# Scan rows of 16 channels by eight states, third-order permutation at the sums, and scores in 32x128 tiles

## The chip, the cores and the metric

The kernel runs on one core of a Trainium2 chip. The metric is the device time of one execution in microseconds (us), from the first to the last instruction. The engines run their own instruction streams in order and wait for each other by semaphores: PE (TensorE, matmuls; PEld are its weight loads), DVE (VectorE), ACT (ScalarE), POOL (GpSimd) and SP, which only issues DMA transfers. All data is fp32, and an fp32 matmul appears in the trace as two passes, each with a weight load.

## The reference, cut to what matters

Two layers act on `x` of 4 images of 64 x 64 tokens with 128 channels. Layer 0 adds a selective scan (Mamba) in three orders of the tokens: forward, backward, and a "sliced" order in which 16 slices of 256 tokens are interleaved. Layer 1 adds an attention block of 16 heads of 8 channels, in which queries, keys and values are one and the same tensor, and a mixture of 64 experts in which each expert picks tokens.

```
def selective_scan(u, delta, A, B, C):             # 256 channels d, 16 states n, 4096 tokens
    def step(h, inp):
        u_, de_, b_, c_ = inp
        dA = jnp.exp(de_[..., None] * A)
        h = h * dA + (de_ * u_)[..., None] * b_[:, None, :]
        y = jnp.einsum('bdn,bn->bd', h, c_)
        return (h, y)

def mamba_dir(xz, ...):                            # once for each of the three orders
    x = silu(causal_conv1d(x, conv_w, conv_b))
    ...
    delta = jax.nn.softplus(jnp.einsum('dr,brl->bdl', dt_w, dt_raw) + dt_b[None, :, None])
    y = selective_scan(x, delta, A, Bm, Cm)
    y = y + Dp[None, :, None] * x
    return y * silu(z)

scores = jnp.einsum('bhsd,bhtd->bhst', q, q) / np.sqrt(D)    # 16 heads, 4096 x 4096 tokens, D = 8
attn = jax.nn.softmax(scores, axis=-1)
ctx = jnp.einsum('bhst,bhtd->bhsd', attn, q)
```

## The kernel before, in words

**Inputs of the scan** (`Inputs`). For each image, order and chunk of 1024 tokens, `of_chunk` computes the convolution on PE (L357), the SiLU on ACT (L368), the projections (L380, L399), softplus (ACT for Abs, Relu, Exp and Ln at L404 to L411, one DVE pass at L413 that makes `s`, three matmuls at L419 that add the parts, one DVE add at L421) and `du = delta * u` (L425). It writes `delta`, `du`, `u` and the rows of B and C to DRAM through POOL's queue (L340, L385). For the sliced order it makes a second SiLU in permuted order (L370), so that `u` lies in DRAM as the sums will be needed. L302 permutes the image itself.

**The scan** (`Scans.of_image`). The 256 channels by 16 states of one image do not fit 128 partitions. One *step* `s` takes 8 channels: partition p = 8 n + d holds state n of channel d. A chunk of 1024 tokens has 32 steps (k = 0 to 7, j = 0 to 3), an image has 3 orders x 4 chunks x 32 = 384 steps. Each step

- loads `delta` and `du` of its 8 channels, each repeated over 16 states (L480, 512 KB each, on SP's queue; for image 0 `du` is on ACT's);
- takes exp(delta * A) in place on ACT (L492);
- multiplies `du` by the B rows in place (L498), scans along the tokens with `tensor_tensor_scan` (L501), and multiplies by the C rows back into the `du` tile (L508), all on DVE. In the sliced order (order 2) L508 reads and writes in permuted order;
- copies the last column for the next chunk on POOL (`ends`, L502);
- sums over the states on PE (`total`, L514), with a selection matrix `sel` for each j. Four steps make 32 channels; then `out` adds D * u on DVE (L525) and POOL writes the rows to DRAM (L530, L536, and L539 for order 2).

Loads are emitted two steps ahead (`AHEAD`), exps one, and the sums of a group of four steps in the second and third step of the next group. `delta` has 3 buffers, `du` 8, `h` 3.

**Attention** (`Attention.loop`). One image has 1024 rounds (4 head groups j x 8 query blocks of 512 x 32 key blocks of 128). A round computes the scores of four heads in two pairs. Each pair has its own PSUM tile `s` of two banks, and there are three such tiles. For each head the keys are cut into four blocks of 32, so that a matmul (L829) contracts 32 rows (the other heads are masked off in the queries) and yields 32 of 128 key rows: 16 matmuls in a round, each on a 32x32 tile of the array. ACT takes the exp of each pair (L836), and four matmuls with 32 columns each add the values (L845). Round i emits scores(i + 1), then values(i), and then `beside(i)`.

**What runs beside what.** The order of instructions is written by generators. In the *fill* (L1300 to L1305) the scan of image 0 and the inputs of all four images take turns. Then `opening` reads the sums of image 0 and prepares its attention, with some of image 1's scan. In the loops of images 0 to 2, `beside` inserts the scan of the next image, and what follows and precedes attention for the neighbouring images. The loop of image 3 has only such other work, no scan.

Of the kernel before, what the change touches and what calls it, by code (L numbers as in the profile page):

```python
# [16 lines left out]
P = 128  # L17
# [8 lines left out]
NC = L // T  # L26
NB = DI // 8
# [105 lines left out]
def scan_weights(nc, const, load, load_ps, ident, in_proj_w, out_proj_w, dirs):  # L133
# [16 lines left out]
    for i, d in enumerate(dirs):  # L150
# [26 lines left out]

        w["A"] = const["all"].tile([P, NB], F32, name=f"A{i}")
        a_log = d["A_log"].rearrange("(k d) n -> n d k", d=8)
        for n in range(NS):  # L180
            nc.scalar.dma_start(out=w["A"][n * 8 : n * 8 + 8, :], in_=a_log[n])
        nc.scalar.activation(w["A"], w["A"], AF.Exp)
        nc.vector.tensor_scalar_mul(w["A"], w["A"], -1.0)

# [10 lines left out]
        ws.append(w)  # L195
    return w_z, w_out, ws


class Inputs:
# [3 lines left out]
    def __init__(self, tc, ctx, x, w_z, ws, cols, dram, ident):  # L203
# [20 lines left out]
        nc.vector.tensor_scalar_mul(self.minus, ident, -1.0)  # L224
        self.made, self.sz, self.normed, self.sliced, self.gated = {}, {}, {}, {}, {}
# [101 lines left out]
    def of_chunk(self, b, order, c):  # L327
# [34 lines left out]
        kept = u  # L362
        if order == 2:

            kept = self.piece.tile([P, 2, T], F32, tag="us", name=f"uk_{key}")
        for m in range(2):
            bias = w["conv_b"][:, m : m + 1]
            nc.scalar.activation(u[:, m, :], banks[m], AF.Silu, bias=bias)  # L368
            if order == 2:
                nc.scalar.activation(  # L370
                    kept[:, m, :].rearrange("p (i j) -> p j i", i=SLICES),
                    banks[m].rearrange("p (j i) -> p j i", i=SLICES), AF.Silu, bias=bias,
                )
            self.leave()
        keep("u", kept)
# [37 lines left out]
        nc.vector.tensor_scalar(s, e, 1.0, -1.0, ALU.add, ALU.add)  # L413
# [17 lines left out]
class Scans:  # L431
# [6 lines left out]
    def __init__(self, tc, ctx, ws, ident, bank, dram):  # L438
# [7 lines left out]
        self.sel = const.tile([P, 4, 32], F32, name="sel")  # L446
        nc.vector.memset(self.sel, 0.0)
        for j in range(4):
            nc.vector.tensor_reduce(
                self.sel[:, j, 8 * j : 8 * j + 8], ident.rearrange("p (n d) -> p d n", d=8),  # L450
                mybir.AxisListType.X, ALU.add,
            )
        self.sums, self.steps, self.did = {}, {}, set()

    def of_image(self, b, made, queue=None):
# [8 lines left out]
        def rows_of(order, c):  # L464
            for i, name in enumerate(("B", "C")):
                t = self.rows.tile([P, T], F32, tag=name, name=f"{name}_{b}_{order}_{c}")
                nc.sync.dma_start(out=t, in_=made[b, order, c]["bc"][i].unsqueeze(1).to_broadcast([NS, 8, T]))
                spread[order, c, name] = t
            ends[order, c] = self.small.tile([P, NB], F32, tag="ends", name=f"ends_{b}_{order}_{c}")

        def load(s):
            order, c, k, j = steps[s]
            if k == j == 0:
                rows_of(order, c)
            at = 8 * (4 * k + j)
            for name, bufs in (("delta", 3), ("du", 8)):
                t = self.deep.tile([P, T], F32, tag=name, bufs=bufs, name=f"{name}_{b}_{s}")
                src = made[b, order, c][name][at : at + 8]
                by = queue if queue is not None and name == "du" else nc.sync
                by.dma_start(out=t, in_=src.unsqueeze(0).to_broadcast([NS, 8, T]))  # L480
                tiles[name, s] = t
# [6 lines left out]
        def exp(s):  # L488
            order, c, k, j = steps[s]
            at = 4 * k + j  # L490
            t = tiles["delta", s]
            nc.scalar.activation(t, t, AF.Exp, scale=self.ws[order]["A"][:, at : at + 1])  # L492

        def step(s):
            order, c, k, j = steps[s]
            at = 4 * k + j
            dA, dB = tiles.pop(("delta", s)), tiles["du", s]
            nc.vector.tensor_mul(dB, dB, spread[order, c, "B"])  # L498
            h = self.deep.tile([P, T], F32, tag="h", name=f"h_{b}_{s}")
# [3 lines left out]
            into, C_rows = dB, spread[order, c, "C"]  # L503
            if order == 2:

                into = dB.rearrange("p (i j) -> p j i", i=SLICES)
                h, C_rows = (t.rearrange("p (j i) -> p j i", i=SLICES) for t in (h, C_rows))
            nc.vector.tensor_mul(into, h, C_rows)  # L508

        def total(s, y):  # L510
            order, c, k, j = steps[s]
            hC = tiles.pop(("du", s))
            for g in range(4):
                nc.tensor.matmul(  # L514
                    y[32 * g : 32 * g + 32, : T // 4], self.sel[:, j, :], hC[:, 256 * g : 256 * g + 256],
# [3 lines left out]
        def out(s, y):  # L519
# [3 lines left out]
            o = self.rows.tile([P, T // 4], F32, tag="o", name=f"o_{b}_{s}")  # L523
            into = o[:, ::-1] if order == 1 else o
            nc.vector.scalar_tensor_tensor(  # L525
                into, u, self.ws[order]["D"][:, k : k + 1], y[:, : T // 4], ALU.mult, ALU.add
            )
# [4 lines left out]
            for g in range(4):  # L532
# [4 lines left out]
                else:  # L537
                    n = T // SLICES
                    nc.gpsimd.dma_start(  # L539
                        out=to.rearrange("p (i j) -> p i j", i=SLICES)[:, 4 * g : 4 * g + 4, c * n : (c + 1) * n],  # L540
                        in_=rows.rearrange("p (i j) -> p i j", i=4),
# [57 lines left out]
class Attention:  # L599
# [202 lines left out]
    def loop(self, b, beside):  # L802
# [17 lines left out]
        def scores(i):  # L820
# [3 lines left out]
            for pair in range(2):  # L824
                s_ps = self.ps_s.tile([P, 2, QB], F32, tag="s", name=f"s_{b}_{i}_{pair}")
                for k in range(2):
                    at = 32 * (2 * pair + k)
                    for r in range(0, P, 32):
                        nc.tensor.matmul(  # L829
                            s_ps[r : r + 32, k, :],  # L830
                            qT[at : at + 32, kc * P + r : kc * P + r + 32],
                            queries[j, qb][at : at + 32, :],
                            start=True, stop=True,
                        )
# [566 lines left out]
```

## Time and profile before

The median is 13711.54 us of 3 runs (13687.13 to 13717.04); the profiled execution spans 13701.5 us.

| stage | us from the start | us |
|---|---|---|
| setup, first inputs | 0 to 142 | 142 |
| fill: scan of image 0, inputs of all images | 142 to 2476 | 2334 |
| last inputs, opening of image 0 | 2476 to 2910 | 434 |
| loops of images 0 to 2, beside scans of 1 to 3 | 2910 to 10889 | 7979 |
| loop of image 3 | 10894 to 13251 | 2357 |
| end: experts' answers | 13251 to 13701 | 450 |

| group of the page | count | busy us | mean ns |
|---|---|---|---|
| L836 ACT exp of scores | 8192 | 7909.6 | 1026 |
| L829 PE scores | 131072 | 5364.4 | 605 |
| L845 PE values | 32768 | 4416.3 | 609 |
| L501 DVE scan, with and without `ends` | 1152 + 384 | 2728.5 + 886.9 | 2368, 2310 |
| L508 DVE times C | 1536 | 2288.8 | 1490 |
| L498 DVE times B | 1536 | 1868.9 | 1217 |
| L492 ACT exp of the scan | 1536 | 1771.0 | 1155 |

Busy is the union of a group's records, so records that run side by side count once; the mean is of single records. A matmul's count is in passes, two for each matmul. Moved bytes are 2258 MB, 1611 MB of it the loads of L480.

### The profile page before, as it was taken

The numbers are of one execution on the slowest core, as the hardware profiler recorded it, in microseconds if no ns is written. First come the engines' busy times: TensorE is split into PE (matmuls) and PEld (weight loads), VectorE is DVE, ScalarE is ACT, GpSimd is POOL, SyncE is SP. The second block draws the span as 40 slices with busy tenths as digits, with TensorE's granted clock in tenths as the row PEclk, the third lists the DMA queues.
The fourth block names the chain that finished last, engine by engine and source line by source line (L and its number), as shares of the span: only waits on it lengthen the run. The fifth ranks groups of instructions, "written<-read, shape, count | busy, mean of one in ns | idle before, by whom it ended". The sixth has DMA issues, their size and how long they took to land.

```text
span 13701.5 us, 413290 instructions
## 1 busy us (share of the span) xinstructions
PE 12427.7 (91%) x183559; PEld 3442.8 (25%) x183559; DVE 9363.8 (68%) x8614; ACT 10595.7 (77%) x10743; POOL 3708.4 (27%) x4144
## 2 busy tenths in 40 slices
PE   7787878459999999899999998999999999999976
PEld 3333333212222222222222222222222222222224
DVE  6998999778888976788889767888896210000014
ACT  4555555259999988789999887999998888888861
POOL 2233334222333432223334322233442000000001
PEclk8888888679999999999999999999999999999986
DMA  6999998768888876777777767777775200000015
GB/s 187 264 258 257 264 246 247 211 173 207 203 202 200 193 188 155 192 190 190 192 183 187 182 156 197 188 187 194 184 192 152 63 26 8 10 10 17 27 36 174
DMA packets 916535, 2258.23 MB, mean 165 GB/s; under 512 B 213054, under 2 KB 346486, under 8 KB 914742
## 3 DMA queue, kind: packets, MB, share of 16 engines
q1 hardware_dynamic: 691790, 1712.22, 50.3%
q0 software_dynamic: 138048, 300.78, 6.6%
q10 hardware_dynamic: 84904, 218.78, 6.2%
q8 instruction: 1435, 23.51, 0.8%
q14 instruction: 358, 2.93, 0.1%
HBM read 1922.19 MB, written 308.94 MB: 163 GB/s over the span
## 4 chain that ended last, share of the span: by engine, by line
PE 70%; DVE 16%; DMA 6%; issue 3%; ACT 2%; SPq 1%; POOL 1%; ACTq 0%; DVEq 0%; POOLq 0%
PE s L829 32%; PE acc L845 26%; DVE h L501 6%; PE y L514 3%; DVE du L498 3%; DVE du L508 2%; PE cv L357 2%; DMA delta<-d_delta 1%; PE sp L419 1%; PE h L963 1%; ACT e L836 1%; PE fo L973 1%; DMA y<-d_sz 1%; DMA x<-in_x_dram 1%; PE dt L399 1%
## 5 line engine op out<-in xcount | busy, mean ns | idle before, releaser
L836 ACT ACTIVATE e<-s 128x1024 f32<-128x1024 f32 x8192 | 7909.6, 1026 | 1142.2 <-PE s L829 945.8
L829 PE MATMUL s<-qm,qT 32*32 32x512 f32 x131072 | 5364.4, 605 | 189.4 <-ACT e L836 92.5
L845 PE MATMUL acc<-e,v 128*32 128x512 f32 x32768 | 4416.3, 609 | 40.4 <-ACT av L854 25.0
L502 POOL COPY ends<-h 128x1 f32<-128x1 f32 x1536 | 2157.7, 1405 | 5147.2 <-DVE h L501 5123.3
L501 DVE TENSOR_TENSOR_SCAN h<-delta,ends,du 128x1024 f32<-128x1024 f32 x1152 | 2728.5, 2368 | 401.0 <-ACT delta L492 272.7
L492 ACT ACTIVATE delta<-delta,A 128x1024 f32<-128x1024 f32 x1536 | 1771.0, 1155 | 1138.5 <-DMA delta<-d_delta 1008.9
L508 DVE TENSOR_TENSOR du<-h,C 128x1024 f32<-128x1024 f32 x1536 | 2288.8, 1490 | 52.6
L829 PEld LDWEIGHTS s<-qm,qT 32*32 32x32 f32 x131072 | 1234.5, 103 | 3587.9 <-PE s L829 2503.2
L498 DVE TENSOR_TENSOR du<-du,B 128x1024 f32<-128x1024 f32 x1536 | 1868.9, 1217 | 20.0 <-DMA du<-d_du 20.0
L845 PEld LDWEIGHTS acc<-e,v 128*32 128x32 f32 x32768 | 656.1, 108 | 3537.6 <-issue 3379.7
L514 PE MATMUL y<-du,sel 128*32 128x256 f32 x12288 | 854.3, 399 | 145.4 <-DVE o L525 100.9
L501 DVE TENSOR_TENSOR_SCAN h<-delta,du 128x1024 f32<-128x1024 f32 x384 | 886.9, 2310 | 116.5 <-ACT delta L492 69.7
L860 POOL DMA_DIRECT2D d_ctx<-av x512 | 260.2, 515 | 1615.6 <-ACT av L854 1607.5
L514 PEld LDWEIGHTS y<-du,sel 128*32 128x32 f32 x12288 | 391.5, 114 | 786.7 <-issue 442.2
L357 PE MATMUL cv<-xn,conv 128*128 128x512 f32 x1024 | 496.0, 644 | 46.7 <-DVE xn L294 27.6
L966 DVE TENSOR_SCALAR h<-h,b 128x512 f32<-128x512 f32 x96 | 71.7, 747 | 510.3 <-PE h L963 509.8
L977 DVE TENSOR_TENSOR x1r<-x1r,fo 128x128 f32<-128x128 f32 x128 | 36.2, 284 | 535.0 <-PE fo L973 534.0
L525 DVE SCALAR_TENSOR_TENSOR o<-us,D,y 128x256 f32<-128x256 f32 x384 | 181.6, 473 | 240.0 <-PE y L514 239.8
L419 PE MATMUL sp<-s,minus 128*128 128x512 f32 x384 | 221.8, 662 | 130.8 <-DVE s L413 130.7
L539 POOL DMA_DIRECT2D d_y<-o x512 | 281.4, 556 | 184.4 <-DVE o L525 168.0
L536 POOL DMA_DIRECT2D d_y<-o x512 | 255.9, 506 | 199.8 <-DVE o L525 187.7
L419 PE MATMUL sp<-e,ident 128*128 128x512 f32 x384 | 222.9, 665 | 75.1 <-ACT e L410 43.5
(238 smaller groups left out, 6323.5 us busy)
## 6 DMA issues: line engine op xcount, KB each, us to landing
delta<-d_delta SPq DMA_DIRECT2D x1536, 512.0 KB
du<-d_du SPq DMA_DIRECT2D x1152, 512.0 KB
du<-d_du ACTq DMA_DIRECT2D x384, 512.0 KB
d_delta<-r POOLq DMA_DIRECT2D x48, 1024.0 KB
d_du<-u POOLq DMA_DIRECT2D x48, 1024.0 KB
us<-d_u SPq DMA_DIRECT2D x384, 128.0 KB
y<-d_y SPq DMA_DIRECT2D x192, 256.0 KB
d_u<-u POOLq DMA_DIRECT2D x32, 1024.0 KB
```

The costliest lines, as they stand in the source:

```text
L357: nc.tensor.matmul(ps[:, cut], w["conv"][:, k, m * P : (m + 1) * P], reads(k, g), start=(k == 0), stop=(k == 3))
L419: nc.tensor.matmul(ps[:, cut], sign, t[:, m, cut], start=(i == 0), stop=(i == 2))
L492: nc.scalar.activation(t, t, AF.Exp, scale=self.ws[order]["A"][:, at : at + 1])
L498: nc.vector.tensor_mul(dB, dB, spread[order, c, "B"])
L501: nc.vector.tensor_tensor_scan(h, dA, dB, first, ALU.mult, ALU.add)
L502: nc.gpsimd.tensor_copy(ends[order, c][:, at : at + 1], h[:, T - 1 :])
L508: nc.vector.tensor_mul(into, h, C_rows)
L514: nc.tensor.matmul(y[32 * g : 32 * g + 32, : T // 4], self.sel[:, j, :], hC[:, 256 * g : 256 * g + 256], start=(j == 0), stop=(j == 3),)
L539: nc.gpsimd.dma_start(out=to.rearrange("p (i j) -> p i j", i=SLICES)[:, 4 * g : 4 * g + 4, c * n : (c + 1) * n], in_=rows.rearrange("p (i ...
L829: nc.tensor.matmul(s_ps[r : r + 32, k, :], qT[at : at + 32, kc * P + r : kc * P + r + 32], queries[j, qb][at : at + 32, :], start=True, st ...
L836: nc.scalar.activation(e, s_ps, AF.Exp, scale=1.0 / math.sqrt(D))
L845: nc.tensor.matmul(accs[j, qb][32 * k : 32 * k + 32, :], v[:, kc, h * VW : h * VW + 32], es[i][k // 2][:, k % 2, :], start=(kc == 0), stop ...
```

## The change

A step now takes 16 channels by 8 states: partition p = 8 d + n. Two successive steps (even and odd j) share one load of `delta` and `du`, one step for states 0 to 7 and one for 8 to 15, so that `delta` and `du` are read once for 16 channels by all states. The even step writes exp and du * B to tiles of their own (`dA`, `dB`), the odd one works in place. The rows of B and C come in halves; `A` is laid out for it and loaded after the other weights, half of it on POOL's queue. `h` gets two buffers instead of three.

In the sliced order, the permutation moves from the step (L508) and from the second SiLU (L370) to the sums (L525): 256 columns for 32 channels at once, with runs of 16 instead of 64 elements in the write to DRAM.

The softplus's `s` = (e + 1) - 1 moves from one DVE pass to two ACT passes. The scores of a head are one matmul with 128 columns in place of four with 32. The number of steps, scans, exps and sums stays.

```
-        nc.vector.tensor_scalar(s, e, 1.0, -1.0, ALU.add, ALU.add)
+        nc.scalar.activation(s, e, AF.Identity, bias=1.0)
+        nc.scalar.activation(s, s, AF.Identity, bias=self.minus_one)
...
-            if order == 2:
-                nc.scalar.activation(
-                    kept[:, m, :].rearrange("p (i j) -> p j i", i=SLICES),
-                    banks[m].rearrange("p (j i) -> p j i", i=SLICES), AF.Silu, bias=bias,
-                )
...
-            for name, bufs in (("delta", 3), ("du", 8)):
+            if j % 2:
+                return
+            for name, bufs in (("delta", 3), ("du", 4)):
                 t = self.deep.tile([P, T], F32, tag=name, bufs=bufs, name=f"{name}_{b}_{s}")
-                src = made[b, order, c][name][at : at + 8]
+                src = made[b, order, c][name][at : at + 16]
-                by.dma_start(out=t, in_=src.unsqueeze(0).to_broadcast([NS, 8, T]))
-                tiles[name, s] = t
+                by.dma_start(out=t, in_=src.unsqueeze(1).to_broadcast([16, NS2, T]))
+                tiles[name, s] = tiles[name, s + 1] = t
...
+            if j % 2 == 0:
+                tiles["delta", s] = self.deep.tile([P, T], F32, tag="dA", bufs=2, name=f"dA_{b}_{s}")
+            A = self.ws[order]["A"][:, j % 2, 2 * k + j // 2].unsqueeze(1)
+            nc.scalar.activation(tiles["delta", s], t, AF.Exp, scale=A)
...
+            if j % 2 == 0:
+                tiles["du", s] = self.deep.tile([P, T], F32, tag="dB", bufs=3, name=f"dB_{b}_{s}")
+            dB = tiles["du", s]
+            nc.vector.tensor_mul(dB, du, spread[order, c, "B", j % 2])
+            h = self.deep.tile([P, T], F32, tag="h", bufs=2, name=f"h_{b}_{s}")
...
-            if order == 2:
-                into = dB.rearrange("p (i j) -> p j i", i=SLICES)
-                h, C_rows = (t.rearrange("p (j i) -> p j i", i=SLICES) for t in (h, C_rows))
-            nc.vector.tensor_mul(into, h, C_rows)
+            nc.vector.tensor_mul(dB, h, spread[order, c, "C", j % 2])
...
+            if order == 2:
+                into = o.rearrange("p (i j) -> p j i", i=SLICES)
+                u, y = (t.rearrange("p (j i) -> p j i", i=SLICES) for t in (u, y))
...
-                        out=to.rearrange("p (i j) -> p i j", i=SLICES)[:, 4 * g : 4 * g + 4, c * n : (c + 1) * n],
-                        in_=rows.rearrange("p (i j) -> p i j", i=4),
+                        out=to.rearrange("p (i j) -> p i j", i=SLICES)[:, :, at : at + n],
+                        in_=rows.rearrange("p (i j) -> p i j", i=SLICES),
...
-                    for r in range(0, P, 32):
-                        nc.tensor.matmul(
-                            s_ps[r : r + 32, k, :],
-                            qT[at : at + 32, kc * P + r : kc * P + r + 32],
-                            queries[j, qb][at : at + 32, :],
-                            start=True, stop=True,
-                        )
+                    nc.tensor.matmul(
+                        s_ps[:, k, :], qT[at : at + 32, kc * P : (kc + 1) * P], queries[j, qb][at : at + 32, :],
+                        start=True, stop=True,
+                    )
```

## The prediction

> **What bounds the kernel now.** I read the page's busy tenths first, then busy time by stage, then the waits of DVE and ACT within a stage, then the timeline of single rounds.
>
> ```profile
> ## 2 busy tenths in 40 slices
> PE   7787878459999999899999998999999999999976
> DVE  6998999778888976788889767888896210000014
> ACT  4555555259999988789999887999998888888861
> DMA  6999998768888876777777767777775200000015
> ```
>
> Three stages with three limits. Slices 0 to 6 are the fill: the scan of image 0 beside the inputs of all images, DVE at 9, DMA at 9, ACT half idle. Slices 8 to 31 are attention of images 0 to 2 beside the scans of images 1 to 3: PE at 9, ACT at 8 or 9. The last stretch is attention of image 3 alone: PE at 9, DVE idle. Cut at the scan's first and last step and at the first and last score matmul of the loops:
>
> ```profile
> core 0: us, PE busy (x) PEld busy (x) DVE busy (x) ACT busy (x) POOL busy (x), PEclk, DMA share, GB/s
> 142.00:2476.00 2334.00, 1928.13 (x6475) 770.73 (x6476) 2177.21 (x1448) 1327.86 (x1097) 836.64 (x907) 0.85 0.92 257
> 2476.00:2910.00 434.00, 90.38 (x461) 49.43 (x467) 279.62 (x412) 67.89 (x58) 90.52 (x101) 0.54 0.62 167
> 2910.00:10889.00 7979.00, 7726.07 (x133216) 1874.79 (x133216) 6452.63 (x5605) 7113.30 (x7392) 2568.62 (x2751) 0.98 0.75 183
> 10894.00:13251.00 2357.00, 2345.45 (x41564) 546.61 (x41540) 212.57 (x528) 2001.47 (x2088) 134.70 (x241) 1.00 0.06 18
> ```
>
> Fill: DVE is busy 2177 of 2334 us. In the same window ACT waits 637 us for delta loads, but DVE waits for ACT's exp only 21 us (17.5 plus 3.9): neither the loads nor ACT limit the fill. Loops: the waits of ACT in 2910 to 10889 are
>
> ```profile
> ACT e L836 <- PE s L829: 659.8, 1157, 25.2
> ACT delta L492 <- DMA delta<-d_delta: 99.2, 33, 9.4
> ```
>
> so ACT waits for scores; PE sets the pace, with ACT close behind. How one round runs, in the last loop:
>
> ```profile
> 12003.04 1.16 PE L829 MATMUL s<-qm,qT 32*32 32x512 f32 x32
> 12004.13 0.16 PEld L845 LDWEIGHTS acc<-e,v 128*32 128x32 f32 x8 [0.84 <-issue]
> 12004.13 1.07 PE L845 MATMUL acc<-e,v 128*32 128x512 f32 x8
> 12004.30 1.94 ACT L836 ACTIVATE e<-s 128x1024 f32<-128x1024 f32 x2 [0.46 <-PE s L829]
> ...
> 12005.12 0.29 PEld L963 LDWEIGHTS h<-zT,w 8*128 8x128 f32 x2 [0.84 <-issue]
> 12005.13 1.12 PE L963 MATMUL h<-zT,w 8*128 8x512 f32 x2
> 12006.17 0.23 PEld L829 LDWEIGHTS s<-qm,qT 32*32 32x32 f32 x31 [0.76 <-issue]
> ```
>
> Start to start: 16 score matmuls (32 records, two passes each) take 1.09 us, the four value matmuls 0.99, and one lone 8x128 matmul of 512 columns 1.05. The sixteen ran side by side.
>
> **What the Trainium skill says.** "TensorE: Matmul & The Clock Gate", section "LDWEIGHTS (loading the stationary operand)": the load takes (columns)/1.2 ns, not rows; 32 columns are 27 ns, 128 are 107. The trace agrees in kind: the weight-load records take 103 ns (32 columns) and 182 (128 columns), 79 apart. "TensorEngine Tiling (Array Packing)", section "Key Properties": changing the tiling mode drains the array, different tiles run in parallel. Both hold here: no score phase overlaps a value phase, and the 64x128 tiles of the scatter (L1238), two row groups with 128-column weights, pack 24 records of 272 ns into 1.52 us. Four row groups with 128-column weights no row shows.
>
> ```profile
> 13661.14 1.52 PE L1238 MATMUL sc<-answer,chosen 64*128 64x128 f32 x24
> ```
>
>  "DMA: Bandwidth & Descriptors", "Specifications": below 512 B a transfer is not at line rate.
>
> **The change part by part.**
>
> *Scores, 16 tiles of 32x32 to 4 of 32x128.* The same columns stream through the same four row groups into the same four banks. Gone are 12 of 16 starts, spaced about 7 ns (0.12 us over a phase, because 32 weight loads spread over 0.25 us at 103 each). New is 80 ns more of exposed weight load at each mode switch. So a whole phase becomes the lone matmul's 1.05 plus three starts of 7 to 20 ns: 1.07 to 1.11, against 1.09. But half the rounds are split: the second pair waits for the exp that frees its PSUM slot. The weight-load timeline shows such a gate, the second pair's loads at 11101.83 and the values at 11102.85, 1.02 us later; with 128-column weights that is 1.06.
>
> ```profile
> 11101.83 0.18 PEld L829 LDWEIGHTS s<-qm,qT 32*32 32x32 f32 x16
> 11102.85 0.16 PEld L845 LDWEIGHTS acc<-e,v 128*32 128x32 f32 x8 [0.84 <-issue]
> ```
>
>  The first pair's exp, which starts 1.26 us after the phase (12003.04 to 12004.30), starts 0.04 later too. These chase each other. Call d the gate's delay: a round lasts d + 1.02 + 1.00 (values); the gate of the next round opens at 1.26 + 1.02 (the exp) + 0.05 (to the weights) after this round's start, so the next d is 0.31 - d. Two rounds take 4.04 + 0.31, 2.17 each; two stretches of four rounds near 11110 us with nothing in between measure 2.174. After: each d sums to 1.30 + 1.02 + 0.05 - 2.06 = 0.31 again, two rounds take 4.12 + 0.31, 2.215 each: +0.04. That is 1024 x 0.043 = 44 us in the last loop, taken at the middle of the spacing. In the other loops scan exps (0.4 to 0.47 a round) hold the gate more often than PE does, so I take about half, 3072 x 0.023 = 71. Sum: **+115 us**, 80 to 145.
>
> *Third order permuted at its sums.* In the fill L508 takes 1225 ns in orders 0 and 1 (first line, 142 to 1667 us; min, median, max), and in the third (second line, 1680 to 2470 us) 1915 on average:
>
> ```profile
> L508 DVE TENSOR_TENSOR du<-h,C x247: 1224/1225/1228, 144.4 to 1661.0; 128x1024 f32<-128x1024 f32 x124
> ...
> L508 DVE TENSOR_TENSOR du<-h,C x121: 1224/1941/2235, 1681.7 to 2461.1; 128x1024 f32<-128x1024 f32 x121
> ```
>
> 128 steps of image 0 x 0.69 = 88 us of DVE in the fill. L525 now writes strided instead, 32 x 256 elements; at the same 0.67 ns an element, 6 us back. L370 (32 x 2.05 us of ACT) goes, ACT not being a limit there. In the loops the same DVE saving (about 0.8 x 384 = 300 us) is hidden: rounds 448 to 800 of the first loop, which hold order 2, run 2.45 to 2.51, no slower than order 0. The writes of L539 fall from 256 to 64 B runs, 512 descriptors per 32 KB instead of 128. L536 (32) takes 506 ns, L539 556, L340 (256) 724: I take 0.8 us, up to 1.5, on a POOL that is a third busy. Who waits there are the `ends` copies, and with h on two buffers scan s+2 waits for copy s; the margin now is 6.8 us or more in three quarters of the fill's steps and 2.4 at the least. A few us.
>
> *softplus' s to ACT.* L413 leaves DVE: 48 x 1.218 = 58 us of fill. ACT gets two passes of about 1.91 us (L411's row, same shape), 183 us on an engine that is idle 1000; Copy, Abs and Relu bring no table load of their own in this trace and I expect none for Identity. PE waited 125 us for DVE's s; ACT runs ahead of DVE there, so this wait should not grow.
>
> Fill sum: 88 + 58 - 6 = 140 us of DVE. The chain through the fill is DVE for about 45% but PE (cv, sp, dt) for nearly a third, so not all of it reaches the end: I take **-120**, from -60 to -160.
>
> *One load for two steps.* delta and du loads halve (1536 + 1536 of 512 KB, 1.6 GB, to 0.8), B and C loads double (96 to 192): about 2258 to 1500 MB. The multiplies, scans and exps keep number and size; even steps write to dA and dB. delta can now be loaded five steps ahead of its scan instead of three, and SP stands less at the head of its queue (it waits 1944 us for scans in the fill). Gain where something waited for loads: of ACT's 99 us in the loops I take **-40**; in the opening, 434 us of y loads queued behind deltas (73 us of DVE waits), **-30**, ends 0 and -70 for each. New wait: the multiply of step s+6 needs the third dB, which PE's sum of step s frees. Laid on the old trace, that comes too late 4 times in the fill (8 us) and about 35 times an image later (40 us of a DVE with slack). With startup (A's 96 small loads, half on POOL, now ahead of the inputs) I book **+10**.
>
> Sum: -120 - 40 - 30 + 115 + 10 = -65: **13645 us**.
>
> **Rivals.**
>
> 1. *Weight loads of the four row groups queue up* (slower). One load of 107 ns behind another delays each pair by 0.11 more, so two rounds by about 0.3: 4096 x 0.15 = +615 on top of the forecast's 13645: about 14260. For: nothing shows four groups at once. Against: L1238 shows two fully parallel.
> 2. *The fill gains little and the score phase costs its 145* (the chain hangs on PE; POOL's small writes hold up the copies): -60 + 145 - 30 = +55: 13765. For: PE's third of the chain.
> 3. *Half the DMA traffic is worth more*: the loads' relief takes 80 in the loops and 70 in the opening, fill -160, scores at their low end (+80): -230, 13480. For: 0.92 DMA share in the fill. Against: DVE hardly waits for it.
>
> **How the numbers follow.** Forecast's neighbourhood 0.5, rival 3 0.18, rival 2 0.2, rival 1 0.12. Low end 13480 from rival 3; the high end, 13840, takes rival 2 with some of the unknowns of POOL and row groups and leaves rival 1 out. Faster by over 27 us: most of the first, all of rival 3: 0.62. Within: 0.14. Slower: 0.24.
>
> **What would show it.** Right: fill from first scan step to last about 2210 us; third-order L508 back at 1.22; score phase start to start 1.07 to 1.11, the last loop about 2.34 us a round against 2.30; DMA share in the loops near 0.45 with no change of pace. Wrong: score phases of 1.3 or more (rival 1), or a last loop faster than 2.28; `ends` or dB waits of DVE over 50 us; ACT idle behind delta as before.

## The result, and the profile after

The changed kernel takes 13409.7 us (median of 4 runs, 13401.1 to 13416.1) against 13714.3 before: a ratio of 0.9782, 95% interval 0.9765 to 0.9799. That is 305 us less, where 65 were predicted: the direction was right, and the time lies below the range.

The busy tenths of the page after (40 slices of the span):

```profile
## 2 busy tenths in 40 slices
PE   7797978369999999999999999999999999999976
...
DVE  6998989678888877888888679888884210000014
ACT  5665656269999998899999889999998888888851
...
DMA  5666666544444444544444545444443100000015
```

The reader is to see what has not changed: PE at 9 through all loops, ACT just below. DMA, at 6 to 9 before, is at 4 to 6, and the dips of PE in the middle of the loops (the 8s of before) are gone. Now the stages, cut at the scan of image 0 and at the first score matmuls of the loops (us, busy times, granted clock, DMA share, GB/s):

```profile
core 0: us, PE busy (x) PEld busy (x) DVE busy (x) ACT busy (x) POOL busy (x), PEclk, DMA share, GB/s
151.00:2460.00 2309.00, 1917.03 (x6619) 771.83 (x6623) 2111.43 (x1451) 1480.38 (x1190) 806.77 (x937) 0.86 0.64 185
2460.00:2810.50 350.50, 51.29 (x284) 34.41 (x276) 211.30 (x361) 33.24 (x27) 62.29 (x71) 0.52 0.47 126
2810.50:10590.00 7779.50, 7647.42 (x59556) 2264.13 (x59556) 6194.95 (x5607) 7104.78 (x7395) 2354.25 (x2751) 0.99 0.45 115
10590.00:12948.00 2358.00, 2347.90 (x16992) 674.12 (x16994) 212.49 (x528) 2001.16 (x2089) 134.91 (x241) 1.00 0.05 16
```

The same cuts serve every kernel below. *Start* ends at the first scan, *fill* at the start of image 0's last scan (2544 us in the kernel before, a little after the cut of its table), *opening* at the first score matmul, *loops* runs from there to the first score matmul of image 3, and *last loop* to its last value matmul.

| kernel | start | fill | opening | loops | last loop | median us | ratio to before, 95% |
|---|---|---|---|---|---|---|---|
| before | 142 | 2402 | 364 | 7986 | 2361 | 13714.3 | 1 |
| changed | 151 | 2310 | 350 | 7779 | 2362 | 13409.7 | 0.9782 [0.9765, 0.9799] |
| e1_scores_only | 143 | 2416 | 366 | 7927 | 2362 | 13663.3 | 0.9959 [0.9947, 0.9972] |
| e3_sums_only | 142 | 2350 | 367 | 7974 | 2365 | 13663.2 | 0.9964 [0.9951, 0.9976] |
| e4_loads_and_sums | 142 | 2290 | 353 | 7816 | 2358 | 13415.0 | 0.9779 [0.9766, 0.9792] |
| e2_all_but_scores | 149 | 2316 | 352 | 7812 | 2361 | 13440.7 | 0.9798 [0.9784, 0.9811] |
| e10_s_on_act | 151 | 2518 | 365 | 7977 | 2360 | 13825.9 | 1.0090 [1.0076, 1.0104] |
| e7_s_on_dve | 141 | 2292 | 349 | 7785 | 2359 | 13379.0 | 0.9757 [0.9744, 0.9770] |
| e5_load_each_step | 150 | 2504 | 368 | 7957 | 2361 | 13801.5 | 1.0062 [1.0049, 1.0074] |
| e14_four_deltas | 151 | 2386 | 368 | 7837 | 2362 | 13553.1 | 0.9881 [0.9864, 0.9897] |
| e6_two_deltas | 149 | 2403 | 349 | 7805 | 2362 | 13514.4 | 0.9857 [0.9843, 0.9870] |
| e12_spare_traffic | 150 | 2312 | 359 | 7791 | 2363 | 13443.2 | 0.9809 [0.9796, 0.9823] |
| e13_split_loads | 155 | 2339 | 368 | 7804 | 2362 | 13475.6 | 0.9829 [0.9814, 0.9844] |
| e8_h_of_64_rows | 146 | 2319 | 348 | 7792 | 2368 | 13417.6 | 0.9782 [0.9768, 0.9795] |
| e9_delta_on_pool | 143 | 2416 | 344 | 8204 | 2360 | 13908.7 | 1.0153 [1.0140, 1.0167] |
| e11_s_dve_delta_pool | 140 | 2294 | 338 | 7831 | 2362 | 13415.6 | 0.9796 [0.9782, 0.9809] |

Stages are read from one profiled execution each. Three pairs of kernels differ only in `s`, which is computed before the loops begin (before and e10_s_on_act, e4_loads_and_sums and e2_all_but_scores, changed and e7_s_on_dve): they lie 4 to 9 us apart in the loops. The kernel before, e1_scores_only and e9_delta_on_pool have one and the same fill, and lie up to 14 us apart there. So a single stage difference under some 15 us proves nothing by itself.

The changed kernel's gain is 92 us in the fill, 14 in the opening and 207 in the loops, less 9 at the start, 1 in the last loop and 4 at the end: 299, which is the difference of the two profiled spans. The prediction had a gain of 120 in the fill, 30 in the opening, and for the three shared loops a loss of 71 less 40 = 31. The shared loops are where most of the error lies, 238 us; the last loop, for which +44 was predicted, came out even.

### The profile page after: what moved, and what is told of

It reads as the page before. It is cut to its first block, busy times and chain, and to the rows that moved or that the text cites. A ratio compares the mean times of both kernels' runs of the same rounds, so it can differ in the third digit from the quotient of the medians.

```text
span 13402.9 us, 213892 instructions
## 1 busy us (share of the span) xinstructions
PE 12305.7 (92%) x85255; PEld 3948.9 (29%) x85255; DVE 8969.0 (67%) x8565; ACT 10704.2 (80%) x10807; POOL 3464.3 (26%) x4192
## 5 line engine op out<-in xcount | busy, mean ns | idle before, releaser
L833 PE MATMUL s<-qm,qT 32*128 32x512 f32 x32768 | 5416.6, 642 | 127.9 <-DVE qm L822 76.3
L508 POOL COPY ends<-h 128x1 f32<-128x1 f32 x1536 | 1841.9, 1199 | 5104.7 <-DVE h L507 5088.8
L833 PEld LDWEIGHTS s<-qm,qT 32*128 32x128 f32 x32768 | 1790.0, 183 | 3288.8 <-PE s L833 1438.0
L507 DVE TENSOR_TENSOR_SCAN h<-dA,ends,dB 128x1024 f32<-128x1024 f32 x576 | 1374.5, 2386 | 197.9 <-ACT dA L495 140.9
L507 DVE TENSOR_TENSOR_SCAN h<-delta,ends,du 128x1024 f32<-128x1024 f32 x576 | 1354.1, 2351 | 164.7 <-ACT delta L495 95.5
L495 ACT ACTIVATE dA<-delta,A 128x1024 f32<-128x1024 f32 x768 | 886.8, 1155 | 339.6 <-DMA delta<-d_delta 217.7
L504 DVE TENSOR_TENSOR dB<-du,B 128x1024 f32<-128x1024 f32 x768 | 935.2, 1218 | 211.8 <-PE y L515 193.1
L495 ACT ACTIVATE delta<-delta,A 128x1024 f32<-128x1024 f32 x768 | 886.6, 1154 | 179.4 <-PE y L515 168.8
L509 DVE TENSOR_TENSOR du<-h,C 128x1024 f32<-128x1024 f32 x768 | 940.7, 1225 | 26.3
L509 DVE TENSOR_TENSOR dB<-h,C 128x1024 f32<-128x1024 f32 x768 | 940.7, 1225 | 26.3
L504 DVE TENSOR_TENSOR du<-du,B 128x1024 f32<-128x1024 f32 x768 | 934.2, 1216 | 0.0
L507 DVE TENSOR_TENSOR_SCAN h<-delta,du 128x1024 f32<-128x1024 f32 x192 | 440.1, 2292 | 43.1 <-ACT delta L495 18.7
```

Source lines behind the costliest of these rows:

```text
L495: nc.scalar.activation(tiles["delta", s], t, AF.Exp, scale=A)
L504: nc.vector.tensor_mul(dB, du, spread[order, c, "B", j % 2])
L507: nc.vector.tensor_tensor_scan(h, dA, dB, first, ALU.mult, ALU.add)
L508: nc.gpsimd.tensor_copy(ends[order, c][:, at : at + 1], h[:, T - 1 :])
L509: nc.vector.tensor_mul(dB, h, spread[order, c, "C", j % 2])
L833: nc.tensor.matmul(s_ps[:, k, :], qT[at : at + 32, kc * P : (kc + 1) * P], queries[j, qb][at : at + 32, :], start=True, stop=True,)
```

## Experiments: which part made the loops faster

**The scores alone.** The kernel before with the one matmul of 128 columns for each head:

```
-                    for r in range(0, P, 32):
-                        nc.tensor.matmul(s_ps[r : r + 32, k, :], qT[at : at + 32, kc * P + r : kc * P + r + 32], ...
+                    nc.tensor.matmul(s_ps[:, k, :], qT[at : at + 32, kc * P : (kc + 1) * P], ...
```

> The kernel before with nothing changed but the score matmuls (4 of 32x128 a round for 16 of 32x32). What I predicted of this part, +115 us: 13830 us, of it +44 in the last loop and +71 in the three shared loops. Theory S (the new scores share the mode of the 8x128 FFN matmul h, which then hides in the score phase, 32 times an image at about 1.05 us): the last loop within 10 us of before's 2357, the shared loops together -30 to -100, total 13600 to 13690. Theory L (the loops gained by the paired loads alone): shared loops within 30 us of before's, last loop unchanged, total 13690 to 13750.

Measured: 13663.3 us, the loops 59 us shorter, the last loop unchanged. The predicted +115 is refuted in both its parts, +71 and +44. The numbers are those of theory S, though its mechanism falls below (e8_h_of_64_rows), and they explain less than a third of the loops' 207.

**The sums alone.** The kernel before with the third order permuted at its sums (L508 plain, L525 permuted, no second SiLU):

> The kernel before with the third order permuted at its sums and nothing else: rows, loads, scores and s as before. e4_loads_and_sums shortened the fill by 112 us and the first three loops with their gaps by 170; this tells the share of the sums. Theory L (paired loads made the loops faster): start of loop 0 to start of loop 3 stays within 30 us of before's 7986, fill 60 to 85 us shorter (88 less 6 of DVE, most of it on the path), total 13620 to 13660. Rival D (the 260 us of DVE that the third order frees inside the loops made them faster): loops 100 us or more shorter, total 13450 to 13560.

Measured: fill 52 us shorter, a little under what I had expected, loops 12 us shorter, 13663.2 us. In its loops DVE is busy 6185 us instead of 6455, and that bought nothing there that can be told from the spread. Rival D is refuted.

**Loads and sums, and all but the scores.** The changed kernel with the old scores, once with `s` on DVE as before and once with `s` on ACT:

> The changed kernel with the scores as before (16 of 32x32) and with softplus' s back on DVE: what is left of the change is the layout with one load for two steps and the permutation at the sums. Theory L (loads): shared loops about 150 to 200 us shorter than before's 7960 with gaps, fill 60 to 90 shorter, total 13430 to 13490. Theory S (scores): shared loops within 60 us of before's, total 13570 to 13640. In both the last loop stays at 2357 and the DMA share in the loops is near 0.45.

> The changed kernel with the scores as before (16 of 32x32). Theory L: 13390 to 13440, as the changed kernel or a little above. Theory S: shared loops 100 us or more longer than the changed kernel's, 13500 to 13620. My predicted +115 for the scores, if it were right beside the rest: 13295. Against e4_loads_and_sums it is s on ACT instead of DVE: 58 us of DVE less in the fill, which I had booked as a gain of up to 58; if PE's longer wait for s eats it, the two fills are within 20 us of each other.

Measured: the layout with its paired loads and the sums alone give 13415.0 us, practically the whole gain. Against e3_sums_only the layout with its paired loads is worth 158 us in the loops (7974 to 7816) and 60 in the fill. From e2_all_but_scores to the changed kernel the scores bring another 33 us of loops. Between e4_loads_and_sums and e2_all_but_scores lies `s` alone: +26 us in the fill and 7 at the start, a loss.

## Experiments: what the paired loads take away

**A load for each step again.** The changed kernel, with the new layout, but `delta` and `du` loaded for every step and with the buffers of before; exp and product are again written in place, without `dA` and `dB` (those lines are left out here):

```
-            if j % 2:
-                return
-            for name, bufs in (("delta", 3), ("du", 4)):
+            for name, bufs in (("delta", 3), ("du", 8)):
...
-                tiles[name, s] = tiles[name, s + 1] = t
+                tiles[name, s] = t
```

> The changed kernel, but every step loads its own delta and du again, in place and with 3 and 8 buffers as before; B and C still come in halves. Traffic back above 2250 MB, the lead of delta back to three steps; scores, sums and s stay changed. Theory L: the loops (start of loop 0 to start of loop 3) go back by 120 to 190 us from 7779 to 7900 to 7970, ACT waits for delta again (about 100 us), total 13530 to 13620. Rival D: loops within 30 us of 7779, total 13390 to 13440.

Measured: loops +178, as theory L said. But the fill went back too, by 194 us, to 102 more than before the change: the total missed the expectation by nearly 200. Without the paired loads the other edits together lose.

Where do 178 us of loops lie? The starts of the score phases tell the length of every round. In 512 of the 3072 rounds, those in which one image ends and the next begins (832 to 895, 960 to 1151, 1856 to 1919, 1984 to 2175), e5_load_each_step takes 1505 us and the changed kernel 1377. So 128 of the 178 are in a sixth of the rounds. A *wait* is time in which an engine stands idle before an instruction, put down to what released it (left of the arrow who waits, right of it for whom). Here are ACT's waits in rounds 960 to 1151 (us, times, longest), of the kernel before (5323 to 5905 us) and of the changed one (5194 to 5722):

```profile
ACT e L836 <- PE s L829: 77.6, 78, 14.3
ACT delta L492 <- DMA delta<-d_delta: 39.0, 14, 8.5
```

```profile
ACT e L838 <- PE s L833: 55.3, 70, 11.8
ACT ang L759 <- DVE ang L110: 9.4, 1, 9.4
```

and DVE's waits for the attention's own loads in the same rounds, before and after:

```profile
DVE cT L922 <- DMA part<-d_share: 25.3, 7, 6.1
DVE qm L817 <- DMA qT<-d_q: 22.7, 1, 22.7
DVE sum L907 <- DMA sum<-d_sum: 19.6, 1, 19.6
```

```profile
DVE sum L909 <- DMA sum<-d_sum: 14.2, 1, 14.2
DVE qm L822 <- DMA qT<-d_q: 13.3, 1, 13.3
...
DVE cT L924 <- DMA part<-d_share: 0.4, 1, 0.4
```

Each late delta stops ACT, and the exps of the scores stand behind it on the same engine; the attention's loads are late as well. The reader is to see that 39 of the 99 us of delta waits on which the prediction looked sit in one such stretch, and that ACT's wait for scores and DVE's waits for the attention's loads fall together with them. Which of the two late loads lengthened the wait for scores these lines do not tell.

Is it the bytes, the count, or the moment at which a load may go? Four kernels tell them apart.

**The bytes.** The changed kernel, with every paired load of images 1 to 3 followed by the same 512 KB once more into a DRAM tile that nobody reads:

```
                 by.dma_start(out=t, in_=src.unsqueeze(1).to_broadcast([16, NS2, T]))
                 tiles[name, s] = tiles[name, s + 1] = t
+                if queue is None:
+                    spare = self.spare[name, s // 2 % 4]
+                    nc.sync.dma_start(out=spare, in_=src.unsqueeze(1).to_broadcast([16, NS2, T]))
```

> The changed kernel with spare traffic in images 1 to 3: after each paired delta or du load the same 512 KB are moved once more, from DRAM to a DRAM tile that nobody reads, on the same queue; no buffer is held and no load waits longer at the head of the queue for one. The fill stays as in the changed kernel. Theory B (the loops gained because the rings are half empty): loops (start of loop 0 to start of loop 3) back by 100 us or more, 7880 to 7960, total 13510 to 13600. Theory Q (they gained because half the loads stand at the head of SP's queue waiting for a buffer): within 40 us of 7779, total 13400 to 13450.

Measured: 13443.2 us, loops 7791, +12, opening +9. Its loops' window against that of e5_load_each_step (the last two columns are DMA share and GB/s):

```profile
2820.50:10611.80 7791.30, 7641.52 (x59552) 2263.59 (x59552) 6194.66 (x5607) 7107.47 (x7395) 2359.94 (x2752) 0.99 0.61 191
```

```profile
3022.10:10979.20 7957.10, 7719.54 (x59554) 2275.59 (x59554) 6185.68 (x5607) 7109.16 (x7395) 2359.24 (x2751) 0.98 0.77 187
```

More is moved per second than in e5_load_each_step, at nearly the pace of the changed kernel. So the halved traffic, which is what the change shows most plainly, is not what made the loops faster: with most of it restored they lose 12 us. (The share of the engines is 0.61 and not 0.77, so a limit between the two is not excluded; and the spare loads leave the fill as it was, so for the fill the bytes were not tried.)

**The slack.** e5_load_each_step with one more `delta` tile:

```
-            for name, bufs in (("delta", 3), ("du", 8)):
+            for name, bufs in (("delta", 4), ("du", 8)):
```

> e5_load_each_step (the changed kernel with a load of its own for every step) with four delta tiles instead of three, so that a delta load waits for the scan two steps back and not for the one just before. Theory W (each step's load comes too late because it waits for the scan just before): loops (start of loop 0 to start of loop 3) 7790 to 7860 instead of e5's 7957, no delta waits of ACT there, fill 50 to 100 us below e5's 2504, total 13520 to 13650. Theory N (the number of loads counts): loops within 40 us of 7957, total 13720 to 13800.

Measured: loops 7837, 120 of the 178 us back, and the fill 118 of its 194, at the traffic and count of e5_load_each_step. ACT's delta waits in the loops, of e5_load_each_step and of this kernel:

```profile
ACT delta L491 <- DMA delta<-d_delta: 106.8, 38, 10.4
```

```profile
ACT delta L491 <- DMA delta<-d_delta: 41.3, 12, 7.0
```

In the 512 rounds where images change it takes 1423 us, so most of what came back came back there. The other 58 us of the loops and 76 of the fill stay open; the count of loads and the bytes may have a part in them.

What changed can be read from SP's own queue. Its longest waits in the loops, in us and times, of the kernel before, of e14_four_deltas and of the changed kernel, where L480, L479 and L481 are the same load and `y` is the sum over the states:

```profile
SPq L480 <- DVE h L501: 5020.4, 1102, 17.7
SPq L480 <- PE y L514: 408.8, 287, 4.6
```

```profile
SPq L479 <- DVE h L501: 2878.7, 814, 14.1
SPq L479 <- PE y L509: 2125.5, 452, 10.7
```

```profile
SPq L481 <- PE y L515: 4292.6, 501, 17.3
SPq L481 <- DVE h L507: 1156.5, 295, 17.3
```

The sum is alike: 5429, 5004 and 5449 us of SP standing at a load that has no free tile. What differs is for whom it stands. With three `delta` tiles in place, the load for step s + 2 may go only when the scan of step s - 1 is done, and its exp comes a step later; any hold-up on SP then reaches ACT. In the changed kernel SP mostly stands for the sum that frees a `du` tile. The traces also give the lead itself, from the start of a load's issue to the start of its first exp: its median in the loops is 13.5 us in the kernel before and in e5_load_each_step, 18.5 in e14_four_deltas and 23.7 in the changed kernel (23.1 with the spare traffic). For `du`, up to its product with B, it is 13.5 us before and 16.9 in the changed kernel.

**Two delta tiles, and split loads.** The changed kernel with two paired `delta` tiles instead of three, and with each paired load issued as two of 64 rows:

> The changed kernel with two delta tiles of the pair instead of three: the traffic of the changed kernel, but a delta is loaded at most three steps ahead of its exp. If the loops gained by less traffic and shorter queues: within 20 us of the changed kernel, 13390 to 13430. If they gained by the longer lead of delta: ACT waits for delta again by 50 to 100 us in the loops, total 13460 to 13580.

> The changed kernel with each paired load split into two of 64 rows into the same tile: as many delta and du loads as before the change, the bytes and the buffers of the changed kernel. Theory W: loops within 30 us of 7779, total 13400 to 13450. Theory N: loops 80 us or more longer, total 13490 or more.

Measured: two tiles cost 26 us in the loops, but 93 in the fill. Split loads cost 25 in the loops, 29 in the fill and 18 in the opening. In the loops the split loads keep within theory W's 30 us, though their total lies above its range: the count is not the main cause, but it costs something. With two tiles ACT waits 36 us for delta in the loops, less than the 50 to 100 of the second theory. SP there stands 5352 us for scans, and the median lead of a delta is back at 13.5 us, but only every second step needs one; that this is why two tiles do little harm in the loops is a reading, not shown by itself. In the fill, where DVE is the bound and takes 6.0 us a step (2310 us for 384 steps; in the loops one comes every 6.75), the third tile is needed: ACT waits 366 us for delta there, against 37 in the changed kernel. The total lies in the middle of the second range I gave, but for a reason in another stage.

**Another queue.** The kernel before with the delta loads of images 1 to 3 on POOL's queue:

```
-                by = queue if queue is not None and name == "du" else nc.sync
+                by = nc.sync if queue is not None or name == "du" else nc.gpsimd
+                if queue is not None and name == "du":
+                    by = queue
```

> The kernel before, with the delta loads of images 1 to 3 issued on POOL's queue instead of SP's; nothing else moves and the traffic stays at 2258 MB. e5_load_each_step put the loops' gain to the paired loads. Theory Q (a delta load that waits for a buffer stands at the head of SP's queue, and the small loads of the attention stand behind it): loops (start of loop 0 to start of loop 3) 100 to 160 us shorter than before's 7986, DVE's waits for part, sum and un shorter, total 13560 to 13630. Theory B (the rings are too busy, whatever the queue): within 40 us of 7986, or longer by POOL's own work at each issue, total 13680 to 13800. The fill, where image 0 is loaded as before, stays at 2402.

Measured: loops +218. The attention's loads did come earlier (DVE's waits for `part`, 50 us before, are 11), but ACT's waits for delta grew from 99 to 326 us. That this is because POOL issues them in order with work of its own is argued, not shown.

```profile
ACT e L838 <- PE s L831: 625.5, 1145, 25.6
ACT delta L494 <- DMA delta<-d_delta: 326.3, 133, 15.6
```

It doesn't decide between Q and B, and it shows what late deltas cost: 227 us more of waiting, 218 us of loops, about one for one, with the attention's loads earlier beside it. The wait for scores, 660 us in these loops before, did not grow with them.

## Experiments: softplus' s, and the FFN matmul

**s on ACT alone.** The kernel before with only this edit:

> The kernel before with softplus' s on ACT in two passes, nothing else. My prediction booked 58 us of DVE saved in the fill and PE's wait for s (131 us) unchanged: 13655 to 13715. What the runs so far say (PE's s wait was 292 us in e5_load_each_step, where delta still is loaded for each step and ACT stands waiting for it before it gets to s; fills of 2504 there and 2350 in e3_sums_only): fill 80 to 150 us longer than 2402, PE's wait for s about 300, total 13790 to 13870.

Measured: fill +116, 13825.9 us. The waits of the fill (151 to 2669 us) of e10_s_on_act, where L415 is the second pass and L494 the scan's exp:

```profile
ACT delta L494 <- DMA delta<-d_delta: 517.1, 109, 11.5
...
PE sp L421 <- ACT s L415: 275.5, 44, 10.6
```

```profile
DVE r L423 <- PE sp L421: 131.3, 38, 7.5
DVE h L503 <- ACT delta L494: 64.2, 32, 4.7
```

and PE's and DVE's waits of the fill before:

```profile
PE sp L419 <- DVE s L413: 130.7, 30, 15.9
```

```profile
DVE r L421 <- PE sp L419: 33.4, 16, 4.9
```

PE waits for `s` 276 us where it waited 131, and DVE waits for PE 131 us where it waited 33. The DVE is the fill's bound, and it got back as waiting more than the 57 us of work that it lost. Why `s` comes later has two possible parts. The two passes are longer: 1.90 and 2.00 us, where DVE took 1.22. And ACT stands 517 us for deltas (640 before, when `s` was not in its order), which can push the passes back in its order. Laid over the trace, ACT is not idle while PE waits: of the 276 us it spends 155 in the two passes themselves, 72 in exps of the scan and their table loads and 33 in the part that makes `z`. So the length of the passes is the larger part that shows. That late deltas add to the loss is seen from another pair: where the loads are paired and ACT's delta waits in the fill are 37 us, the same edit costs 26 us of fill and not 116.

**The changed kernel with s on DVE.**

> The changed kernel with softplus' s back on DVE, one pass instead of ACT's two. e4_loads_and_sums against e2_all_but_scores put s on ACT at +26 us in the fill. If that holds beside the new scores: fill about 2290 instead of 2310, loops within 15 us of 7779, total 13375 to 13395, below the changed kernel. My prediction's reading (s on ACT saves up to 58 us of the fill): 13430 to 13470.

Measured: 13379.0 us (13378.1 to 13388.6), below every run of the changed kernel. Fill 2292, start 141. DVE's waits there:

```profile
DVE o L530 <- PE y L514: 34.0, 13, 5.8
DVE r L415 <- PE sp L413: 15.9, 6, 3.6
...
DVE h L506 <- ACT dA L494: 5.2, 3, 1.7
```

PE's wait for `s` is 189 us here, about that of the changed kernel (203), and yet DVE waits less: ACT, busy 1305 us and not 1480, delivers the exps in time (DVE waits 5 us for them, 35 in the changed kernel), and DVE's waits for the sums and for PE's `sp` are 24 and 16 us shorter. The 9 us at the start, which I had booked on the reordered loads of `A`, are gone too, and e10_s_on_act has them without that reordering: they were the first chunk's `s`. This is the best kernel of the study; it keeps everything of the change but this edit.

**h in another tiling mode.** In the changed kernel the FFN's first matmul (L965, 8x128) runs among the score matmuls, since both take 32 rows by 128 columns; before, it was a phase of its own. A stretch of the last loop:

```profile
12017.72 0.69 PE L965 MATMUL h<-zT,w 8*128 8x512 f32 x1
...
12017.73 0.70 PE L833 MATMUL s<-qm,qT 32*128 32x512 f32 x3
...
12018.25 0.59 PE L965 MATMUL h<-zT,w 8*128 8x512 f32 x1
...
12018.27 1.44 PE L833 MATMUL s<-qm,qT 32*128 32x512 f32 x5
...
12019.63 0.16 PEld L847 LDWEIGHTS acc<-e,v 128*32 128x32 f32 x8 [0.76 <-issue]
```

So e8_h_of_64_rows pads the matmul with zero rows:

```
-        self.w1 = const.tile([D, FFN], F32, name="w1")
+        self.w1 = const.tile([64, FFN], F32, name="w1")
...
-            zT = self.piece([D, 512], "p0", name=f"zT_{b}_{g}")
+            zT = self.piece([64, 512], "p0", name=f"zT_{b}_{g}")
```

> The changed kernel with the FFN's first matmul h padded by zero rows from 8x128 to 64x128, so that it can't share the scores' row groups; the padding costs two small memsets and no further matmul. Theory S (h hides in the score phase because both are of 32x128): the 128 h matmuls run as phases of their own again, 30 to 45 us more in the last loop (2390 to 2400) and as much in each shared loop, total 13530 to 13590. Rival (h's place does not matter, the last loop's predicted +44 was an error of the round model): within 20 us of the changed kernel, 13390 to 13430.

Measured: 13417.6 us, last loop +6, loops +13. The h matmuls are phases of 1.05 us again, but theory S is refuted: h with a whole score phase takes 1.91 us together (12017.72 to 12019.63) against 1.05 + 1.07 apart, 0.2 us saved 32 times, which is the 6 us. The 13 us of the loops are within what the stages differ anyway.

**Both at once.** e7_s_on_dve with the paired deltas of images 1 to 3 on POOL's queue:

> The changed kernel with s on DVE (as e7_s_on_dve) and the paired delta loads of images 1 to 3 on POOL's queue. Theory Q: some of SP's 260 us at the head for delta in the rounds where images change is left in the changed kernel; 10 to 40 us less in the loops than e7_s_on_dve's 7785, total 13335 to 13370. Theory B: within 10 us of e7_s_on_dve or a little slower, 13370 to 13400.

Measured: 13415.6 us, 46 us of loops worse than e7_s_on_dve, with 93 us of delta waits that are not there otherwise, so here a wait cost half its length. Neither theory's number: POOL's queue costs here as well.

## Why the prediction was right in direction and wrong in size

- **The steps that failed**: two terms of the sum, the loads (out by 118 us) and the scores (by about 150). The first is "Gain where something waited for loads: of ACT's 99 us in the loops I take -40". It is mis-sized: the layout with paired loads measured -158 in the loops (e3_sums_only to e4_loads_and_sums), and e5_load_each_step +178 when the pairing is taken out. I took a wait of ACT at less than its own length, since PE sets the pace. Between these two kernels ACT's delta waits fall from 78 us to under 1, so even their whole length is half of the 158. At the same time a term falls that I had put at nothing in the loops: the attention's loads that queue behind the deltas, which I booked for the opening only, where -30 became -14. DVE's waits for them (`y`, `qT`, `un`, `part`, `sum`) go from 401 to 272 us. That these make up the rest is argued, not shown: no kernel changes them alone. The runs that change the deltas' queue do not show that a late delta costs more than its own length: 227 us more of delta waits cost 218 in e9_delta_on_pool, 93 cost 46 in e11_s_dve_delta_pool. The reason that I gave ("delta can now be loaded five steps ahead of its scan instead of three, and SP stands less at the head of its queue") was half right: the slack of the delta load is the cause of 120 of the 178 us, from one tile, but SP stands as long as before. Most of the bytes, put back, cost 12 us of loops.
- **Scores, +115**: the second term, wrong in sign in the shared loops (-33 beside the rest and -59 alone, for +71) and at nothing in the last (+1 for +44). The score phase is as predicted, 1.07 us ungated and 1.30 gated, where before had 1.09 and 1.27. What failed is "The first pair's exp, which starts 1.26 us after the phase, starts 0.04 later too". In the changed kernel's last loop:

```profile
11601.85 1.14 PE L833 MATMUL s<-qm,qT 32*128 32x512 f32 x8
...
11602.92 1.07 PE L847 MATMUL acc<-e,v 128*32 128x512 f32 x8
11603.08 4.01 ACT L838 ACTIVATE e<-s 128x1024 f32<-128x1024 f32 x4 [1.45 <-PE s L833]
...
11603.92 1.37 PE L833 MATMUL s<-qm,qT 32*128 32x512 f32 x8
...
11605.22 1.07 PE L847 MATMUL acc<-e,v 128*32 128x512 f32 x8
...
11606.21 1.14 PE L833 MATMUL s<-qm,qT 32*128 32x512 f32 x8
```

The exp starts 1.23 us after the phase (11601.85 to 11603.08), 0.02 to 0.03 earlier than before (median of the last loop: 1.24 for 1.25). Why is not shown: the last pass of the first pair starts 0.54 us after the phase, where before it was 0.50, so the 0.04 is there, but the exp follows that pass sooner, after 0.70 us for 0.75. In my own sum d is then 1.23 + 1.02 + 0.05 - 2.06 = 0.24, and two rounds take 4.12 + 0.24 = 4.36. They measure 4.36 (11601.85 to 11606.21), against 2 x 2.174 = 4.35 before: +0.01 for two rounds. The last loop comes out even, with 6 us from h in it. Why the scores gain 33 to 59 us in the shared loops was not tried by itself. At most 13 of them are h, and the earlier first exp, in rounds in which ACT is the later one, would work in that direction. This is argued, not shown.
- **Rival 1** (weight loads of four row groups queue up) is refuted by the same lines: no score phase of 2 us. The Trainium skill's "TensorE: Matmul & The Clock Gate", section "LDWEIGHTS (loading the stationary operand)", on which the 80 ns of the prediction rested, agrees with the trace in the difference: the weight-load records take 183 ns now and took 103.
- **Fill, -120**: -92 measured, but by other terms. I had 88 less 6 for the third order, 58 for `s`, nothing for the loads. The third order gave 52 (e3_sums_only), the layout with paired loads 60 more (e4_loads_and_sums, where I had written "neither the loads nor ACT limit the fill"), and `s` cost 26. "This wait should not grow" failed where `s` alone was moved: PE's wait for it went from 131 us to 276. In the changed kernel it is 203, but 189 with `s` on DVE, so there DVE's other waits carry the loss, those for exps above all (35 us for 5). The L508 of before did come back to its plain time (L509 after, all three orders: min, median, max ns):

```profile
L509 DVE TENSOR_TENSOR dB<-h,C x192: 1203/1225/1228, 153.0 to 2457.0; 128x1024 f32<-128x1024 f32 x192
L509 DVE TENSOR_TENSOR du<-h,C x191: 1219/1225/1227, 157.8 to 2451.6; 128x1024 f32<-128x1024 f32 x191
```

  DVE is busy 131 us less in the fill (2243 to 2111), near the 140 predicted. It idles 38 us more. That a bound is busy for less is an upper end for the gain, and the waits that an edit puts ahead of it come off.
- **The costs I had feared** were near: the +10 booked on the start came out as +9, but by luck, since `s` and not the loads of `A` made it; the third dB costs DVE 8.0 us of waits in the fill, as laid on the old trace; POOL's writes of 64-byte runs take 0.66 us each instead of 0.56, and no wait for them shows.
- **Rival 3** named the place (loads' relief of 80 in the loops, fill of 160) and had half the size in the loops. For the loops its reading, the traffic, is what e12_spare_traffic speaks against, up to the engines' share of 0.61; for the fill, where the share was 0.92 before, the bytes were not tried.

## What to carry to other kernels

Ask of a load not only how busy the rings are but for whom its queue stands. If it may go only once the step just before has finished, each hold-up in that queue reaches the engine that needs it; one more tile, or one load for two steps, buys slack, and the bytes may be the lesser part of such an edit. A wait of an engine that runs close behind the bound, and feeds it, is not to be discounted because the bound is another: here late deltas cost between half and all of their own length. And count every load that stands in the same queue, not only those on which the wait shows first. For work moved from the bound to an engine "with idle time", compare how long it takes there and what it stands behind in that engine's order, not only the idle time: 57 us of DVE moved to an ACT that was half idle cost 116 us alone, and 26 even with the loads paired.

## What the runs showed of the hardware

- Matmuls of 8 rows by 128 columns and of 32 rows by 128 columns run among each other without a switch of phase: 1.91 us for two passes of h and a score phase, against 2.12 apart. The same matmul with 64 rows is a phase of its own, 1.05 us.
- ACT's Identity for 128x2048 takes 2.00 us with its bias from a tile (47 records in the changed kernel's fill, 2001 to 2005 ns) and 1.90 with the constant 1.0 (1892 to 1902 ns); no table load goes with it.
- For nearly the same bytes a second the DMA engines were less busy where part of the transfers went from DRAM to DRAM: 191 GB/s at a share of 0.61 in e12_spare_traffic, 187 at 0.77 in e5_load_each_step.
